# Attention then graph attention on one core: products with reciprocals last in a beat of the first element, finishes from the fourth-last chunk, two places for the rows of bv

## The chip, the cores and the metric

The kernel runs on one core of a Trainium2 chip. The metric is the device time of one execution in microseconds (us), the median of the runs; lower is better. The core has five engines that run side by side and wait for each other by semaphores: TensorE (PE, matmuls), VectorE (DVE), ScalarE (ACT), GpSimd (POOL) and SyncE (SP), which here issues every DMA. Each engine works through its instructions in the order in which the program wrote them.

## The reference

Two layers over x of shape 8 x 2048 x 256 with one 2048 x 2048 adjacency matrix. The first is attention with 4 heads of 64, in which the softmax runs within each chunk of 256 keys and the 8 chunks are added; the second is graph attention; each ends in a residual and a layer norm.

```python
# layer 0
scores = einsum('bhnd,bhjcd->bhnjc', q, kc) / sqrt(Dh)
scores = clip(scores, -10, 10)
scores = where(mask == 0, -10, scores)
attn = softmax(scores, axis=-1)              # within a chunk of 256 keys
ctx = einsum('bhnjc,bhjcd->bhnd', attn, vc)  # summed over the 8 chunks
out = layernorm(ctx @ Wo.T + bo + x) * gamma + beta
x = layernorm(x + out)
# layer 1
e = leaky_relu(s_i[:, :, None] + s_j[:, None, :], 0.2)
attention = softmax(where(mask, e, -inf), axis=-1)
x = layernorm(x + elu(attention @ Wh))
```

## The kernel before

Everything is written in float32, with the order of the instructions set by hand: an engine executes what the Python code emits, in that order.

**Tiling.** An element of the batch has 4 blocks of 512 queries, a block has 8 chunks of 256 keys, a chunk two halves of 128 keys. The main loop (L900) runs over the 256 chunks J; each half of a chunk is a *beat*, so there are 512 beats and some more for the end. An element is 64 beats.

**One beat.** `begin_beat` emits the steps of the second layer that are under way; then come the scores of the beat (L882, PE, into PSUM), the clip with the mask (L893, DVE, in place in PSUM), the exponential (L897, ACT). The scores of the next beat's first pair of heads are already emitted in this beat when there is room. Then follow the matmuls with the values for the chunk *before* (L948): in the chunk's first half the sums of the exponentials (part 2, `ds`) and the first half of the values, in its second half the rest. ACT copies them out of PSUM (L956 to `un`, L962 to `ds`). Last comes `end_beat`.

**The reciprocals' way.** `ds` goes by DMA to a narrow tile `dc` (L964), DVE takes the reciprocal (`inverse`, L970), it goes to DRAM (`rd`, L972) and back over all partitions (`spread`, `r`, L976). Then `scaled` multiplies: for chunk 0 DVE writes ctxT (L981), for the others DVE multiplies `un` in place (L983) and POOL adds it to ctxT (L984). These three are put into `agenda` for the beats in which they fall due: in the first element `inverse` and `spread` one beat after the matmuls and `scaled` four beats after them, later at once and two beats after. `un` has two places, and every third chunk of the first element uses the tile `hr` in addition.

**end_beat (L842).** Before the change, in the first element (beat < 64) and after beat 512, it first calls what is due in `agenda`, in the order in which it was put there; then it emits the products of the second layer and advances each generator in `ahead` and `fins` by one step; then it calls what is left in `agenda`. In between, so in elements 1 to 7, all that is due comes behind the generators.

**The generators.** In the first element `fins` holds the projections of keys and values, `weights_made` (L234), `masks_made` (L163), which turns the adjacency into int8 masks on DVE (L154, L157, diagonal blocks L161) and ACT (L155), and `far_made` (L193; L201, L204), which makes a bfloat16 table for the second layer. `fin` (L342) finishes a block: it loads x (L346) and in its next beat lets POOL add the biases (L349 y, L350 x); when the block's eight chunks are in ctxT (`ctx_done`), in a later beat, come the projection by Wo (L357, L364), statistics (L316 to L322), `normalize` (L329), gamma and beta (L370, L371, on DVE for the very last block), a second norm, a store and a transposition (L383). `fin` is put into `fins` by `scaled` of the chunk NCH - 3, the third-last. The prelude of the second layer for an element (L475) takes maxima over the far table (L438, DVE), with loads of 256 KB (L430). Steps of the second layer use L714 and L727 (ACT), L718 and L723 (DVE, L723 with the int8 mask), L736 (POOL) and L746 (PE). Queries for the next block are loaded (`xT_q`, L120) at the end of the second beat of chunk 6 of a block.

**bv.** In `weights_made`, bv is multiplied through Wo by two matmuls (L247) whose stationary operand is a tile `bvr` filled from bv (L246); both use the tag `hr`, which has one place.

Of the kernel before, what the change touches and what calls it, by code (L numbers as in the profile page):

```python
# [9 lines left out]
F32 = mybir.dt.float32  # L10
# [9 lines left out]
P = 128  # L20
# [8 lines left out]
def tile_adj_attention__then__gat(  # L29
# [42 lines left out]
    NIB = N // IB  # L72
    TPB = IB // P
    NPAIR = H // 2
    NCH = N // CHUNK
# [11 lines left out]
    one = ctx.enter_context(tc.tile_pool(name="one", bufs=1))  # L87
# [146 lines left out]
    def weights_made():  # L234

        for n in range(2):
            for k in range(KC):
                wa = one.tile([P, F], F32, tag="hr", name=f"wa{n}_{k}")
                nc.vector.tensor_mul(wa, W_aug[:, k, 0:F], a_bc[n])
                nc.vector.reduce_sum(W_aug[:, k, F + n : F + n + 1], wa, axis=AX.X)  # L240
            yield

        pb = ps_m.tile([P, F], F32, tag="m", name="pb")
        for k in range(KC):
            rep = one.tile([P, P], F32, tag="hr", name=f"bvr{k}")
            nc.vector.tensor_scalar(rep, ones, bv_c[:, k : k + 1], None, ALU.mult)  # L246
            nc.tensor.matmul(pb, rep, WT["o"][:, k, :], start=(k == 0), stop=(k == KC - 1))  # L247
        nc.vector.scalar_tensor_tensor(bo_bc, pb, float(NCH), bo_bc, ALU.mult, ALU.add)
# [439 lines left out]
    total = B * NIB * NCH  # L688
# [116 lines left out]
    agenda = {}  # L805
    beat = 0
# [6 lines left out]
    def at(when, fn):  # L813
        agenda.setdefault(when, []).append(fn)
# [27 lines left out]
    def end_beat():  # L842

        nonlocal weighted
        if beat < 2 * NIB * NCH or beat >= 2 * total:
            for fn in agenda.pop(beat, []):
                fn()
        for s in weighted:
            s.product()
        weighted = []  # L850
        for gens in (ahead, fins) if beat < 2 * total else (fins, ahead):
            for g in list(gens):
                if next(g, g) is g:
                    gens.remove(g)
        for fn in agenda.pop(beat, []):
            fn()
# [8 lines left out]
    qT = make_qT(0, 0, xT_kv[0, 0])  # L865
    fins.append(projections())
    fins.append(weights_made())
    fins.append(masks_made())
    fins.append(far_made())
# [30 lines left out]
    for J in range(total + 1):  # L900
        b, ib, j = J // (NIB * NCH), J // NCH % NIB, J % NCH
# [4 lines left out]
        for half in range(2):  # L906
# [30 lines left out]
            if prev is not None:  # L937
                if half == 0:

                    pool, tag = (one, "hr") if early and J % 3 == 2 else (two, "un")  # L940
                    prev["un"] = pool.tile([P, 2, IB], F32, tag=tag, name=f"un{prev['name']}")
                for part in ((2, 0), (1,))[half]:
                    m = ps_m.tile([P, IB], F32, tag="m", name=f"u{prev['name']}_{part}")
                    for i in range(2):
                        pc = 2 * prev["j"] + i
                        for h in range(H):
                            f0 = h * D + part * DH
                            nc.tensor.matmul(  # L948
                                m[h * DH : (h + 1) * DH, :],
                                prev["v"][pc // TPB][:, pc % TPB, f0 : f0 + DH] if part < 2 else ones[:, 0:DH],  # L950
                                prev["es"][2 * i + h // 2][:, h % 2, :],
                                start=(i == 0),
                                stop=(i == 1),
                            )
                    if part < 2:
                        nc.scalar.copy(prev["un"][:, part, :], m)  # L956
                    else:

                        ds = two.tile([P, IB], F32, tag="ds", name=f"ds{prev['name']}")
                        nc.scalar.copy(ds, m)  # L962
                        dc = two.tile([P, IB // DH], F32, tag="dc", name=f"dc{prev['name']}")
                        nc.sync.dma_start(  # L964
                            out=dc, in_=ds.rearrange("(h m) (n w) -> h m n w", m=DH, n=DH)[:, 0, :, :]
                        )
                        prev["dc"] = dc

                        def inverse(p=prev):
                            nc.vector.reciprocal(p["dc"], p["dc"])  # L970
                            p["rd"] = dram3.tile([H, IB], F32, tag="rd", name=f"rd{p['name']}")
                            nc.sync.dma_start(out=p["rd"].rearrange("h (m w) -> (h m) w", m=DH), in_=p["dc"])  # L972

                        def spread(p=prev):
                            p["r"] = two.tile([P, IB], F32, tag="r", name=f"r{p['name']}")
                            nc.sync.dma_start(out=p["r"], in_=p["rd"].unsqueeze(1).to_broadcast([H, DH, IB]))  # L976

                        def scaled(p=prev):
                            r2 = p["r"].unsqueeze(1).to_broadcast([P, 2, IB])
                            if p["j"] == 0:  # L980
                                nc.vector.tensor_mul(p["ctxT"], p["un"], r2)  # L981
                            else:
                                nc.vector.tensor_mul(p["un"], p["un"], r2)  # L983
                                nc.gpsimd.tensor_add(p["ctxT"], p["ctxT"], p["un"])  # L984
                            if p["j"] == NCH - 1:
                                ctx_done[p["b"], p["ib"]] = beat
                            if p["j"] == NCH - 3:
                                fins.append(fin(p["b"], p["ib"], p["ctxT"]))

                        lag = 1 if early else 0  # L990
                        at(beat + lag, inverse)
                        at(beat + lag, spread)
                        at(beat + 2 + 2 * lag, scaled)

            end_beat()
            if half == 1:

# [8 lines left out]
    while agenda or fins or ahead or l1_live or l1_open():  # L1006
        begin_beat(1.0)
        middle_of_beat()
        end_beat()
        beat += 1  # L1010
# [44 lines left out]
```

## Time and profile before

| what | value |
|---|---|
| median of 3 runs | 4391.52 us (4390.94 to 4396.86) |
| the profiled execution, whole | 4386.54 us |
| its span, first to last instruction | 4384.7 us |
| mean granted TensorE clock | 0.979 |
| L983, product, 224 times | 277.2 us busy, mean 1238 ns |
| L984, POOL's addition, 224 times | 567.9 us busy, mean 2535 ns |

By stage, from the table of busy times by window:

| us of the span | PE busy | DVE busy | POOL busy | granted clock |
|---|---|---|---|---|
| 0 to 480 (480) | 430.85 | 335.53 | 115.75 | 0.96 |
| 480 to 1000 (520) | 495.21 | 409.99 | 228.15 | 0.99 |
| 1000 to 1527 (527) | 501.88 | 417.81 | 233.78 | 0.99 |
| 2585 to 3114 (529) | 501.80 | 418.39 | 233.59 | 0.99 |
| 4120 to 4385 (265) | 182.43 | 214.56 | 54.18 | 0.85 |

How to read the lines that follow. In a timeline a row gives the start and the length in us, the engine, the source line, the operation, the tile written and those read, how often, and in brackets the engine's idle time before it with what ended it. In a table of groups the columns are busy us, mean ns of one, and idle us before with the releasers. The chain of waits is followed back from the last instruction to what released each step. A tile's buffer number is left out. PE's records are modelled to overlap, so a busy PE isn't PE at its peak. PEld is the weight load on PE. Line numbers are those of the kernel before.

### The profile page before, as it was taken

How to read it: one execution, taken by the hardware profiler on the slowest of the kernel's cores; microseconds unless marked ns; L12 is line 12 of the kernel's file. 1: busy time of each engine (PE TensorE's matmuls, PEld its weight loads, DVE VectorE, ACT ScalarE, POOL GpSimd, SP SyncE). 2: the span in 40 equal slices, each digit the busy share in tenths (PEclk: the TensorE clock that was granted, in tenths of full speed). 3: DMA queues.
4: the chain of work that ended last, by engine and by line, in shares of the span. 5: the costliest groups of instructions: out<-in, count | busy, mean ns of one | idle time of the engine just before them, and what ended most of it. 6: DMA issues, size and time to landing. Idle time of an engine off the chain costs nothing.

```text
span 4384.7 us, 61166 instructions
## 1 busy us (share of the span) xinstructions
PE 4055.8 (92%) x23053; PEld 1913.0 (44%) x23053; DVE 3417.1 (78%) x4530; ACT 2555.5 (58%) x3842; POOL 1759.3 (40%) x901
## 2 busy tenths in 40 slices
PE   8889989999899999999899998999989999899767
PEld 3223334454345534454344543445434454344456
DVE  5876589965898668976699766996579965888777
ACT  5655556665566556666566665566556665555546
POOL 0222235543455434444245442554325542354420
PEclk9999999999999999999999999999999999999889
DMA  5554232223332133321333223222232222322321
GB/s 163 172 174 149 73 114 86 84 72 95 93 97 82 56 108 102 100 75 47 108 103 98 74 74 105 83 95 80 72 105 84 89 78 65 117 83 81 123 73 58
DMA packets 257642, 415.63 MB, mean 95 GB/s; under 512 B 85441, under 2 KB 120513, under 8 KB 256449
## 3 DMA queue, kind: packets, MB, share of 16 engines
q1 hardware_dynamic: 257344, 411.71, 30.7%
q8 instruction: 181, 2.97, 0.3%
q14 instruction: 117, 0.95, 0.1%
HBM read 340.66 MB, written 68.88 MB: 93 GB/s over the span
## 4 chain that ended last, share of the span: by engine, by line
PE 57%; DVE 23%; ACT 7%; DMA 7%; issue 5%; POOL 1%; SPq 0%; DVEq 0%; ACTq 0%; POOLq 0%
PE u L948 17%; PE sc L882 14%; PE us L746 12%; DVE sc L893 6%; DVE fb L438 3%; DVE w L718 3%; PE pv L275 3%; PE pk L256 3%; ACT e L897 3%; DMA dc<-ds 2%; PE pq L256 2%; DVE w L723 2%; PE po L357 2%; PE pw L398 2%; PE us L761 1%
## 5 line engine op out<-in xcount | busy, mean ns | idle before, releaser
L893 DVE SCALAR_TENSOR_TENSOR sc<-sc,mk 128x1024 f32<-128x1024 f32 x1024 | 1205.8, 1222 | 523.1 <-PE sc L882 375.0
L897 ACT ACTIVATE e<-sc 128x1024 f32<-128x1024 f32 x1024 | 1032.7, 1021 | 951.8 <-DVE sc L893 926.5
L882 PE MATMUL sc<-qT,kT 64*128 64x512 f32 x4096 | 1038.7, 622 | 71.8 <-ACT e L897 68.6
L984 POOL TENSOR_TENSOR ctxT<-ctxT,un 128x1024 f32<-128x1024 f32 x224 | 567.9, 2535 | 1135.6 <-DVE un L983 1099.8
L948 PE MATMUL u<-e,v 128*32 128x512 f32 x8192 | 982.8, 597 | 0.0
L746 PE MATMUL us<-wh,w 128*128 128x256 f32 x3584 | 883.0, 396 | 89.5 <-ACT w L727 68.2
L746 PEld LDWEIGHTS us<-wh,w 128*128 128x128 f32 x3584 | 669.8, 194 | 432.5 <-ACT w L727 119.7
L736 POOL TENSOR_TENSOR acc<-acc,w 128x512 f32<-128x512 f32 x392 | 600.0, 1531 | 548.1 <-ACT w L727 537.6
L882 PEld LDWEIGHTS sc<-qT,kT 64*128 64x128 f32 x4096 | 344.3, 186 | 581.3 <-issue 313.7
L718 DVE SCALAR_TENSOR_TENSOR w<-ab,sj,w 128x512 f32<-128x512 f32 x512 | 576.5, 1147 | 6.1 <-ACT w L714 6.1
L948 PEld LDWEIGHTS u<-e,v 128*32 128x32 f32 x8192 | 240.6, 110 | 659.8 <-issue 500.9
L948 PE MATMUL u<-e,ones 128*32 128x512 f32 x4096 | 498.4, 605 | 0.0
L723 DVE TENSOR_TENSOR w<-w,mk 128x512 f32<-128x512 f32 x512 | 458.5, 916 | 45.6 <-DMA mk<-mask 43.1
L438 DVE CUSTOM_DVE_ANT_0 fb<-sj_row,fb 128x1024 bf16<-128x1024 f32 x240 | 383.7, 1609 | 4.5 <-DMA fb<-far 4.5
L956 ACT COPY un<-u 128x512 f32<-128x512 f32 x512 | 300.7, 587 | 108.8 <-PE u L948 100.1
L714 ACT ACTIVATE w<-ab,sj 128x512 f32<-128x512 f32 x512 | 352.3, 715 | 9.9 <-POOL acc L734 5.2
L727 ACT ACTIVATE w<-w 128x512 f32<-128x512 f32 x512 | 308.8, 629 | 83.6 <-DVE w L723 83.2
L983 DVE TENSOR_TENSOR un<-un,r 128x1024 f32<-128x1024 f32 x224 | 277.2, 1238 | 43.6 <-DMA r<-rd 23.1
L948 PEld LDWEIGHTS u<-e,ones 128*32 128x32 f32 x4096 | 107.5, 110 | 352.7 <-issue 286.5
L970 DVE RECIPROCAL dc<-dc 128x16 f32<-128x16 f32 x256 | 63.5, 248 | 149.3 <-DMA dc<-ds 137.3
L962 ACT COPY ds<-u 128x512 f32<-128x512 f32 x256 | 148.6, 580 | 18.5 <-PE u L948 15.5
L357 PE MATMUL po<-WT_o,ctxT 128*128 128x256 f32 x512 | 127.4, 405 | 33.3 <-POOL ctxT L984 29.2
(112 smaller groups left out, 3078.7 us busy)
## 6 DMA issues: line engine op xcount, KB each, us to landing
r<-rd SPq DMA_DIRECT2D x256, 256.0 KB
mk<-mask SPq DMA_DIRECT2D x120, 512.0 KB
fb<-far SPq DMA_DIRECT2D x240, 256.0 KB
xT_k<-in_xT_dram SPq DMA_DIRECT2D x32, 512.0 KB
raw<-in_adjT_dram SPq DMA_DIRECT2D x32, 512.0 KB
rawf<-in_adj_dram SPq DMA_DIRECT2D x32, 512.0 KB
x<-in_x_dram SPq DMA_DIRECT2D x32, 512.0 KB
h_d<-y SPq DMA_DIRECT2D x32, 512.0 KB
```

What stands on the lines that cost most here:

```text
L438: nc.vector.tensor_tensor_reduce(out=fb, in0=row, in1=fb, scale=1.0, scalar=2 * FAR * 0.999, op0=ALU.add, op1=ALU.max, accum_out=dst,)
L714: nc.scalar.activation(self.w, k["ab"][:, 1, :], AF.Identity, bias=k["sj"][:, 1, c : c + 1])
L718: nc.vector.scalar_tensor_tensor(self.w, k["ab"][:, 0, :], k["sj"][:, 0, c : c + 1], self.w, ALU.add, ALU.max)
L723: nc.vector.tensor_tensor(self.w, self.w, self.k["mks"][self.c // HT][:, self.c % HT, :], ALU.min)
L727: nc.scalar.activation(self.w, self.w, AF.Exp)
L736: nc.gpsimd.tensor_add(k["acc"], k["acc"], self.w)
L746: nc.tensor.matmul(k["us"][:, t, :], self.w[:, ts(t, P)], k["wh"][c // TPB][:, c % TPB, 0:F], start=(first and t % 2 == 0), stop=last, ski ...
L882: nc.tensor.matmul(sc[:, h, :], kTs[b][n // TPB][h * D : (h + 1) * D, hp, ts(n % TPB, P)], qT[h * D : (h + 1) * D, hp, :], start=True, sto ...
L893: nc.vector.scalar_tensor_tensor(sc, sc, -CLIP, cap, ALU.max, ALU.min)
L897: nc.scalar.activation(e, sc, AF.Exp)
L948: nc.tensor.matmul(m[h * DH : (h + 1) * DH, :], prev["v"][pc // TPB][:, pc % TPB, f0 : f0 + DH] if part < 2 else ones[:, 0:DH], prev["es"] ...
L984: nc.gpsimd.tensor_add(p["ctxT"], p["ctxT"], p["un"])
```

## The change

Three edits.

1. `end_beat`: in the first element what is due is split. All but `scaled` is called first, as before; the `scaled` that are due go back into `agenda` and are called by the last loop of `end_beat`, behind the generators. After beat 512 nothing changes.
2. `scaled` puts `fin` into `fins` at chunk NCH - 4 (the fourth-last). In elements 1 to 7, and for the last block of the first element, x is loaded and its biases are added two beats sooner; for the other blocks of the first element one beat sooner, since there `scaled` now runs behind the generators. The projection by Wo still waits for `ctx_done`.
3. The second `bvr` tile takes the place `ex` instead of `hr`.

```diff
@@ weights_made
-            rep = one.tile([P, P], F32, tag="hr", name=f"bvr{k}")
+            rep = one.tile([P, P], F32, tag=("hr", "ex")[k], name=f"bvr{k}")
@@ end_beat
-        if beat < 2 * NIB * NCH or beat >= 2 * total:
+        if beat < 2 * NIB * NCH:
+            now = agenda.pop(beat, [])
+            agenda[beat] = [fn for fn in now if fn.__name__ == "scaled"]
+            for fn in now:
+                if fn.__name__ != "scaled":
+                    fn()
+        elif beat >= 2 * total:
             for fn in agenda.pop(beat, []):
                 fn()
@@ scaled
-                            if p["j"] == NCH - 3:
+                            if p["j"] == NCH - 4:
                                 fins.append(fin(p["b"], p["ib"], p["ctxT"]))
```

## The prediction

> **What bounds the kernel now.** I read the page first: its totals and its chain.
>
> ```profile
> PE 4055.8 (92%) x23053; PEld 1913.0 (44%) x23053; DVE 3417.1 (78%) x4530; ACT 2555.5 (58%) x3842; POOL 1759.3 (40%) x901
> ...
> PE 57%; DVE 23%; ACT 7%; DMA 7%; issue 5%; POOL 1%; SPq 0%; DVEq 0%; ACTq 0%; POOLq 0%
> ```
>
> TensorE (PE) carries most of the chain, so a gain has to come out of its idle time or out of the stretches where VectorE (DVE) takes its place. The table of stages says where idle time is: in the first 480 us PE is busy for 430.85 us (49 us idle), in the later elements for about 500 of 527, in the last 265 us for 182. The change touches the first, little of the middle, and the entry to the last.
>
> Second, the groups of the first 520 us, shapes kept apart:
>
> ```profile
> L893 DVE SCALAR_TENSOR_TENSOR sc<-sc,mk 128x1024 f32<-128x1024 f32 x153 | 180.3, 1224 | 95.7 <-PE sc L882 95.1
> ...
> L984 POOL TENSOR_TENSOR ctxT<-ctxT,un 128x1024 f32<-128x1024 f32 x31 | 79.8, 2576 | 296.2 <-DVE un L983 285.5 <-ACT ds L962 10.6
> ...
> L157 DVE TENSOR_SCALAR mb<-raw 128x1024 int8<-128x1024 int32 x32 | 49.9, 1559 | 0.0
> ```
>
> L157 has a median of 0.68 us (its line by itself) and a mean of 1.56, so 49.9 - 32 x 0.68 = 28 us are stretch. The clip L893 never exceeds 1.233 us in 1024 runs. The timeline shows what stretches L157:
>
> ```profile
> 192.40 1.22 DVE L983 TENSOR_TENSOR un<-un,r 128x1024 f32<-128x1024 f32 x1
> ...
> 193.53 0.69 DVE L154 TENSOR_SCALAR mk<-raw 128x1024 int8<-128x1024 int32 x1
> 193.69 2.74 POOL L984 TENSOR_TENSOR ctxT<-ctxT,un 128x1024 f32<-128x1024 f32 x1 [4.67 <-DVE un L983]
> ...
> 194.14 2.85 DVE L157 TENSOR_SCALAR mb<-raw 128x1024 int8<-128x1024 int32 x1
> ...
> 199.04 2.37 DVE L893 SCALAR_TENSOR_TENSOR sc<-sc,mk 128x1024 f32<-128x1024 f32 x2
> ...
> 200.31 1.02 ACT L897 ACTIVATE e<-sc 128x1024 f32<-128x1024 f32 x1 [3.99 <-DVE sc L893]
> ...
> 201.38 2.08 PE L882 MATMUL sc<-qT,kT 64*128 64x512 f32 x4 [3.89 <-ACT e L897]
> ```
>
> The product L983 releases GpSimd's (POOL's) addition L984; the mask instruction behind it ends only when that addition does, 2.17 us late; the next clip is late, its exponential, and PE waits 3.89 us.
>
> **Part 1: products last in a beat, first element.** The instruction lists of the two kernels, built from the code, are the same on PE and ScalarE (ACT). On DVE some 25 products move behind the masks, far rows and statistics of their beat, so the next DVE instructions are the two clips (2.35 us), in whose shadow L984 (2.35 to 2.7 us) fits. What PE idle time goes, by the groups of its gaps that follow a stretched instruction:
>
> - Gaps ending at 196.37 and 201.38 (0.91 + 3.89), one L157 stretched: 2.2. Gaps at 297.53 and 302.30 (0.79 + 3.64), one L157: 2.2.
> - Gaps at 247.81 and 253.85 (0.31 + 4.91): here L154 (2.84), L157 (2.86) and L161 (2.51) are stretched by L349, L350 and L984, 6.4 us in all. Gaps at 350.5 and 354.0 (2.41 + 2.33): L983 (3.30), L154 (2.85), L157 (2.83), again 6.4. The finish now begins one beat sooner there, so L349 and L350 run in a beat that has no mask work; a product or a mask instruction can still meet them. Between 2.2 and the whole gaps (5.2 and 4.7): 3.3 each.
> - Block 0's finish, gaps of 0.76, 1.41 and 0.87 near 139.8 to 156.3: between 0 and 3.0, I take 2.0.
> - The finish of the element's last block moves two beats: PE idles 2.08 us before L357 at 471.17, while POOL goes from L350 (ends 464.3) through two additions. That goes: 2.1.
>
> Sum 2.2 + 2.2 + 3.3 + 3.3 + 2.0 + 2.1 = 15.1.
>
> Behind a gap PE also runs slower:
>
> ```profile
> 245.57 1.92 PE L948 MATMUL u<-e,v 128*32 128x512 f32 x16
> ...
> 253.85 2.08 PE L882 MATMUL sc<-qT,kT 64*128 64x512 f32 x4 [4.91 <-ACT e L897]
> 255.86 3.64 PE L948 MATMUL u<-e,ones 128*32 128x512 f32 x16
> ```
>
> Sixteen matmuls take 3.64 us instead of 1.92; the granted clock is 0.66 in 250 to 260, and 0.57, 0.57, 0.62 behind the other three pairs of gaps. That is about 1.7 us each, 6.9 for four, if all four gaps fall under what triggers it, 0 if none: I take 3.0. The Trainium skill, "TensorE: Matmul & The Clock Gate", Part 1, puts the half rate behind an idle window of about 3.4 us; by that the shortened gaps would cost nothing, the term would be 6.9 and the whole sum 29. The trace disagrees: a gap of 2.08 us is followed by 0.72 over 470 to 476.
>
> Against it: the last product of block 0 now stands behind L154 and L157 (0.63 + 0.67), and PE already waits there for L984 (1.04 us before 161.5): +1.3. The later L984 also frees its `un` place later by up to 4 us; that place is needed a beat and more later (three in turn in this element), so 0; without that cover ACT's copy L956 and PE's `u` would stand still for the same 4 us. The reciprocals L970 keep their place, and so their waits for dc (18.0 us, 7 times).
>
> Another page speaks against the part: "GPSIMD Engine Reference", section 1 (Specifications), says that GpSimd shares its SBUF interfaces with VectorE and collides with two-input instructions, so the moved product itself stays exposed. The trace has it, but seldom (L983 at most 3.37 us, median 1.215); by the rule three such hits would take 3 x 2.1 = 6.3 off, and the sum would be 19.
>
> **Part 2: bv rows.** DVE waits 4.44 us at 35.65 for the first matmul L247. Now its second row is made at once. PE waited 0.38 for it, so 0.4 is gained, and no more, since the DVE sum L248 behind needs both matmuls.
>
> **Part 3: finishes two beats sooner, elements 1 to 7.** Nothing is added; on SP the load of x (512 KB) passes the load of xT_q, and on POOL L349 and L350 pass one L984 and two or three L736. L349 waits for x on POOL (86.3 us, 9 times, after the first element); behind it now stands an L984 whose `un` place ACT writes again 11 us or more after the addition in the trace, so the 5.6 us of L349 and L350 fit, and an L736, which frees one of five `w`.
>
> Block 0 of an element is where PE idles before L357:
>
> ```profile
> 1616.29 3.25 POOL L350 TENSOR_TENSOR x<-x,beta_bc 128x1024 f32<-128x1024 f32 x1
> ...
> 1617.24 3.38 DVE L438 CUSTOM_DVE_ANT_0 fb<-sj_row,fb 128x1024 bf16<-128x1024 f32 x1
> ...
> 1624.07 1.23 DVE L438 CUSTOM_DVE_ANT_0 fb<-sj_row,fb 128x1024 bf16<-128x1024 f32 x1 [1.17 <-DMA fb<-far]
> ...
> 1630.13 6.19 PE L357 MATMUL po<-WT_o,ctxT 128*128 128x256 f32 x15 [4.26 <-POOL ctxT L984]
> ```
>
> Two beats sooner DVE has only clips and small copies, so the stretch of 2.16 us goes. But DVE then waits for the far block instead (its wait of 1.17 grows), so I don't count that. What counts is the x load that now no longer stands in front of dc: DVE waits 1.9, 1.5, 4.1, 1.9, 4.2 us there in the five blocks where the profile names dc, against 1.5 without such a load (546.06): 0.4 + 0 + 2.6 + 0.4 + 2.7 = 6.1, of which I take 4.0. Bounds: 0, and 7 x 2.16 = 15 if the far block isn't the limit.
>
> Blocks 1 to 3: L349 and L350 stretch two L723 (1.4 + 2.2 us) per block, before and after alike, 2 beats apart. PE is busy 129 of 136, 138 of 142, 129 of 133 us there, and covers it: 0. Uncovered, six blocks in the stretch where DVE is busy 15.00 of 15 us would cost 6 x 3.6 = 22; a gain of up to 8 is open too (1.31 us of PE before L357 in six third blocks). Two loads in front of dc: it is issued 5.7 us behind xT_q, x alone lands in 4.1; 0, bound +8.
>
> The last block counts in full, because from 4118 on DVE is the chain:
>
> ```profile
> 4123.48 3.33 POOL L349 TENSOR_TENSOR y<-x,bo_bc 128x1024 f32<-128x1024 f32 x1
> ...
> 4124.54 2.82 DVE L718 SCALAR_TENSOR_TENSOR w<-ab,sj,w 128x512 f32<-128x512 f32 x1
> ...
> 4126.89 2.67 POOL L350 TENSOR_TENSOR x<-x,beta_bc 128x1024 f32<-128x1024 f32 x1
> ...
> 4127.39 2.71 DVE L723 TENSOR_TENSOR w<-w,mk 128x512 f32<-128x512 f32 x1
> ```
>
> Against medians of 0.74 and 0.68 that is 2.1 + 2.0 = 4.1. Two beats sooner DVE sits idle for 6.60 us (before L408 at 4108.88) and PE is the chain, which covers both. I take 4.0; bounds 0, and 5 with the 1.3 us by which x delays dc there (3.06 us in the chain against some 1.8).
>
> **Sum.** -15.1 - 3.0 + 1.3 - 0.4 - 4.0 - 4.0 = -25.2 us. The profiled execution took 4386.5 (span 4384.7), which gives 4361.3. The median of the runs is 4391.5, 5.0 above it, so the forecast for the runs is 4366.
>
> **Rivals.** No change that can be told (within 8.8 us, 0.2%): the gaps refill. For it: PE also waits for xT_q (3.9 + 2.9 + 1.8) and DVE for dc in the first element, and neither moves; two 2.2 us terms, bv and half the tail remain, less 1.3: about -6, 4386. Against it: at 199 to 201 no other releaser is close behind the clip. Larger gain: every group of gaps with its slow clock (5.2 + 4.7 + 4.8 + 4.4 + 3.0 + 2.1 + 6.9 = 31), 15 in the first blocks, 5 at the end: -50, 4341. Slower: L349 and L350 of the second blocks land in the full DVE stretch of the third (22 us), while the first element gives only 4: +18, 4409; it decides from the point where clips, not PE, end last there. For it: DVE 15.00 of 15 in three slices; against: PE is 15.00 in the same ones. That products don't move is excluded by the lists.
>
> **Chances.** Forecast (a gain of 9 to 38 us) 0.58, larger 0.13, no change 0.16, slower 0.13: faster 0.71, same 0.16, slower 0.13. The forecast's own range is 4354 to 4382; to leave out no more than 2 in 10 I take 4338 to 4397.
>
> **What would show it.** L157's mean in the first 520 us near 0.7 with L984 under L893; PE's waits for ACT e in the first 480 us down from 24.1 to about 10; the clock there above 0.96; L718 and L723 unstretched near 4120; the wait before L357 in first blocks hardly smaller. It is wrong if L983 is stretched instead, or if PE's idle time in the third blocks grows.

## The result, and the profile after

The changed kernel is slower, by little: 4398.82 us (4392.37 to 4406.95, 22 runs) against 4393.18 us (4382.87 to 4397.04, 22 runs) of the kernel before on the same chip, a ratio of 1.0015 (95% interval 1.0008 to 1.0021). The forecast was 4366, faster. The profiled execution took 4397.48 us, its span is 4395.7 (before 4386.54 and 4384.7).

The page of the changed kernel, its totals and chain, shows how little the whole says:

```profile
PE 4059.2 (92%) x23053; PEld 1918.3 (44%) x23053; DVE 3376.7 (77%) x4530; ACT 2557.7 (58%) x3842; POOL 1754.2 (40%) x901
...
PE 56%; DVE 22%; ACT 8%; DMA 8%; issue 5%; POOL 1%; SPq 0%; DVEq 0%; ACTq 0%; POOLq 0%
```

DVE is busy 40 us less (3417.1 before): much of the stretch is gone, and the kernel is not faster for it. Where the time went is read by stages. Each column below is a difference between starts of clips in the timeline: up to the first clip of element 1, from there to its second block, from there to the fourth block of element 7, and from there to the end (0.3 us ahead of the span's, in every run). From `end_beat` on the changed kernel's line numbers are seven higher: L983 is now L990 (product), L984 L991, L970 L977, L956 L963, L893 L900, L897 L904.

| us | first element | first block of el. 1 | to block 4 of el. 7 | rest | end |
|---|---|---|---|---|---|
| before | 442.6 | 111.4 | 3425.0 | 405.5 | 4384.4 |
| changed | 433.3 | 116.5 | 3442.7 | 402.8 | 4395.4 |
| difference | -9.3 | +5.2 | +17.7 | -2.7 | +11.0 |

These are one execution each; the medians differ by 5.6. The first element and the last block gained, and everything between lost.

**First element.** The groups of DVE in the first 520 us of the changed kernel (busy us, mean ns | idle before):

```profile
L990 DVE TENSOR_TENSOR un<-un,r 128x1024 f32<-128x1024 f32 x31 | 41.9, 1353 | 7.0 <-DMA r<-rd 7.0
L157 DVE TENSOR_SCALAR mb<-raw 128x1024 int8<-128x1024 int32 x32 | 26.1, 816 | 0.0
```

DVE's wait for dc in the same stretch (us, times, longest), changed kernel first, then the kernel before:

```profile
DVE dc L977 <- DMA dc<-ds: 36.8, 17, 5.0
```

```profile
DVE dc L970 <- DMA dc<-ds: 21.5, 9, 3.4
```

L157 fell from 1559 to 816 ns, and the product is hardly stretched in its stead (in the first 480 us its mean was 1319 ns and is 1367). But DVE now waits 15.3 us longer for dc. Why that costs is seen at the place which the prediction priced with 0.79 + 3.64 us, in the timeline of the changed kernel:

```profile
297.03 0.25 DVE L977 RECIPROCAL dc<-dc 128x16 f32<-128x16 f32 x1 [2.49 <-DMA dc<-ds]
297.20 0.63 DVE L154 TENSOR_SCALAR mk<-raw 128x1024 int8<-128x1024 int32 x1
...
297.75 0.68 DVE L157 TENSOR_SCALAR mb<-raw 128x1024 int8<-128x1024 int32 x1
...
299.28 2.35 DVE L900 SCALAR_TENSOR_TENSOR sc<-sc,mk 128x1024 f32<-128x1024 f32 x2
...
303.96 1.94 PE L383 MATMUL pt<-ident,y 128*128 128x128 f32 x8 [4.68 <-ACT ds L969]
```

No mask instruction is stretched, but the reciprocal in front of them waits 2.49 us for its DMA, the clip comes at 299.28, and PE waits 4.68 us, a step later than before and for ACT's copy L969. So one wait takes the place of another: in the first 450 us PE's waits for ACT's `e` fell from 24.1 to 9.2 us, while those of L383 for ACT's copy `ds` rose from nothing to 6.9 and those of L357 for POOL from 1.0 to 3.9.

**Start of element 1.** Timeline of the changed kernel:

```profile
439.08 2.34 POOL L349 TENSOR_TENSOR y<-x,bo_bc 128x1024 f32<-128x1024 f32 x1 [11.15 <-DMA x<-in_x_dram]
441.50 2.34 POOL L350 TENSOR_TENSOR x<-x,beta_bc 128x1024 f32<-128x1024 f32 x1
443.80 2.34 POOL L991 TENSOR_TENSOR ctxT<-ctxT,un 128x1024 f32<-128x1024 f32 x1
446.17 0.58 ACT L963 COPY un<-u 128x512 f32<-128x512 f32 x1 [8.68 <-POOL ctxT L991]
446.81 3.78 PE L256 MATMUL pk<-xT_k,WT_k 128*128 128x512 f32 x4 [6.38 <-ACT un L963]
```

POOL waits 11.15 us for x, which was issued at 431.54 and landed 7.5 us later. The addition L991 stands behind; ACT's copy waits 8.68 us for its `un` place, PE 6.38 for ACT. Before, L349 came behind that addition (459.46), and ACT waited 3.01. By beat 2 of element 1, 8.15 of the 9.3 us are lost.

**Elements 1 to 7.** In beat 15 of blocks 1 and 2 (counted from 0) of most elements 1 to 4 us are lost. One of them:

```profile
2773.56 2.35 POOL L349 TENSOR_TENSOR y<-x,bo_bc 128x1024 f32<-128x1024 f32 x1 [1.85 <-PE u L955]
2774.45 4.80 DVE L723 TENSOR_TENSOR w<-w,mk 128x512 f32<-128x512 f32 x2
...
2775.99 2.71 POOL L350 TENSOR_TENSOR x<-x,beta_bc 128x1024 f32<-128x1024 f32 x1
...
2782.20 2.35 DVE L900 SCALAR_TENSOR_TENSOR sc<-sc,mk 128x1024 f32<-128x1024 f32 x2
...
2785.50 0.58 ACT L963 COPY un<-u 128x512 f32<-128x512 f32 x1
...
2786.13 3.29 PE L256 MATMUL pq<-xT_q,WT_q 128*128 128x512 f32 x4 [2.14 <-ACT un L963]
```

Two L723 take 4.80 us next to the two additions (1.28 at 2767.20 in the kernel before). DVE has no pause from there to the clip at 2782.20, so the clip, the exponentials and ACT's copy behind them are late, and PE waits in front of the next queries; the four matmuls behind the wait take 3.29 us instead of 1.98. Over the run the matmuls of L256 waited 36.0 us for ACT's copy `un` (27 times), in the kernel before 12.4 (19); 6.4 of it is the wait at the start of element 1.

**Last block.** L349 and L350 left the two instructions that the prediction named, but met another L723, and the next addition met an L718:

```profile
4114.97 3.46 DVE L723 TENSOR_TENSOR w<-w,mk 128x512 f32<-128x512 f32 x2
4115.50 2.37 POOL L349 TENSOR_TENSOR y<-x,bo_bc 128x1024 f32<-128x1024 f32 x1 [2.67 <-DMA x<-in_x_dram]
...
4135.18 3.38 POOL L991 TENSOR_TENSOR ctxT<-ctxT,un 128x1024 f32<-128x1024 f32 x1 [2.08 <-DVE un L990]
4136.26 2.85 DVE L718 SCALAR_TENSOR_TENSOR w<-ab,sj,w 128x512 f32<-128x512 f32 x1
```

### The profile page after: what moved, and what is told of

Same layout as the page of the kernel before. It is cut to its first block, busy times and chain, and to the rows that moved or that the text cites. A ratio compares the mean times of both kernels' runs of the same rounds, so it can differ in the third digit from the quotient of the medians.

```text
span 4395.7 us, 61109 instructions
## 1 busy us (share of the span) xinstructions
PE 4059.2 (92%) x23053; PEld 1918.3 (44%) x23053; DVE 3376.7 (77%) x4530; ACT 2557.7 (58%) x3842; POOL 1754.2 (40%) x901
## 4 chain that ended last, share of the span: by engine, by line
PE 56%; DVE 22%; ACT 8%; DMA 8%; issue 5%; POOL 1%; SPq 0%; DVEq 0%; ACTq 0%; POOLq 0%
PE u L955 17%; PE sc L889 14%; PE us L746 12%; DVE sc L900 6%; DVE w L718 3%; DMA dc<-ds 3%; DVE fb L438 3%; PE pk L256 3%; DVE w L723 3%; ACT e L904 3%; PE pv L275 2%; PE po L357 2%; PE pq L256 2%; PE pw L398 2%; DMA mk<-mask 2%
## 5 line engine op out<-in xcount | busy, mean ns | idle before, releaser
L900 DVE SCALAR_TENSOR_TENSOR sc<-sc,mk 128x1024 f32<-128x1024 f32 x1024 | 1206.2, 1222 | 513.4 <-PE sc L889 367.4
L904 ACT ACTIVATE e<-sc 128x1024 f32<-128x1024 f32 x1024 | 1032.1, 1020 | 931.6 <-DVE sc L900 906.4
L991 POOL TENSOR_TENSOR ctxT<-ctxT,un 128x1024 f32<-128x1024 f32 x224 | 557.8, 2490 | 1110.5 <-DVE un L990 1092.3
L736 POOL TENSOR_TENSOR acc<-acc,w 128x512 f32<-128x512 f32 x392 | 598.7, 1527 | 546.8 <-ACT w L727 536.8
L718 DVE SCALAR_TENSOR_TENSOR w<-ab,sj,w 128x512 f32<-128x512 f32 x512 | 572.9, 1140 | 6.2 <-ACT w L714 6.1
L723 DVE TENSOR_TENSOR w<-w,mk 128x512 f32<-128x512 f32 x512 | 452.9, 906 | 42.8 <-DMA mk<-mask 40.2
L438 DVE CUSTOM_DVE_ANT_0 fb<-sj_row,fb 128x1024 bf16<-128x1024 f32 x240 | 368.5, 1545 | 25.0 <-DMA fb<-far 25.0
L963 ACT COPY un<-u 128x512 f32<-128x512 f32 x512 | 300.6, 587 | 119.9 <-PE u L955 104.2
L714 ACT ACTIVATE w<-ab,sj 128x512 f32<-128x512 f32 x512 | 351.9, 713 | 11.4 <-POOL acc L734 5.5
L990 DVE TENSOR_TENSOR un<-un,r 128x1024 f32<-128x1024 f32 x224 | 278.7, 1244 | 43.7 <-DMA r<-rd 26.3
L977 DVE RECIPROCAL dc<-dc 128x16 f32<-128x16 f32 x256 | 63.6, 248 | 162.5 <-DMA dc<-ds 159.0
L357 PE MATMUL po<-WT_o,ctxT 128*128 128x256 f32 x512 | 133.1, 419 | 43.1 <-POOL ctxT L991 43.1
L256 PE MATMUL pq<-xT_q,WT_q 128*128 128x512 f32 x248 | 126.3, 646 | 38.3 <-ACT un L963 28.4
```

Source lines behind the costliest of these rows:

```text
L256: nc.tensor.matmul(pm, WT[name][:, k, ts(o, P)], xt[:, k, :], start=(k == 0), stop=(k == KC - 1))
L438: nc.vector.tensor_tensor_reduce(out=fb, in0=row, in1=fb, scale=1.0, scalar=2 * FAR * 0.999, op0=ALU.add, op1=ALU.max, accum_out=dst,)
L714: nc.scalar.activation(self.w, k["ab"][:, 1, :], AF.Identity, bias=k["sj"][:, 1, c : c + 1])
L718: nc.vector.scalar_tensor_tensor(self.w, k["ab"][:, 0, :], k["sj"][:, 0, c : c + 1], self.w, ALU.add, ALU.max)
L723: nc.vector.tensor_tensor(self.w, self.w, self.k["mks"][self.c // HT][:, self.c % HT, :], ALU.min)
L736: nc.gpsimd.tensor_add(k["acc"], k["acc"], self.w)
```

## The experiments

All compute the whole reference. T is the beat in which a finish (of blocks 0 to 2 of the first element) loads x in the kernel before; the changed kernel does so at T-1.

| kernel | first element: due last, finish | el. 1 to 7 | first element | first block | middle | rest | ratio to before (95%) |
|---|---|---|---|---|---|---|---|
| before | nothing, T | before | 442.6 | 111.4 | 3425.0 | 405.5 | 1 |
| changed | products, T-1 | early | 433.3 | 116.5 | 3442.7 | 402.8 | 1.0015 (1.0008 to 1.0021) |
| e1_last | products, T+1 | before | 453.2 | 109.2 | 3421.1 | 405.9 | 1.0020 (1.0011 to 1.0029) |
| e2_fin4 | nothing, T-2 | early | 431.2 | 109.0 | 3441.2 | 402.7 | 1.0005 (0.9996 to 1.0014) |
| e4_el0 | products, T-1 | before | 433.0 | 110.8 | 3419.8 | 405.0 | 0.9971 (0.9960 to 0.9983) |
| e5_hold | products, T-1 | x early | 434.1 | 108.4 | 3415.1 | 404.3 | 0.9961 (0.9948 to 0.9973) |
| e8_lastT | products, T | before | 439.1 | 110.9 | 3426.7 | 404.6 | 0.9984 (0.9975 to 0.9993) |
| e9_oldT1 | nothing, T-1 | before | 434.0 | 109.0 | 3428.4 | 405.0 | 0.9984 (0.9975 to 0.9993) |
| e6_un | products, T-1 | early | 432.4 | 107.8 | 3437.9 | 403.1 | 0.9999 (0.9988 to 1.0010) |
| e10_both | nothing, T-2 | x early | 437.3 | 108.8 | 3416.2 | 404.9 | 0.9964 (0.9951 to 0.9978) |
| e11_alllast | all, T-1 | x early | 419.1 | 108.5 | 3416.7 | 406.5 | 0.9915 (0.9902 to 0.9929) |
| e12_tail | products, T-1 | x early, last block early | 434.6 | 108.4 | 3416.6 | 405.2 | 0.9945 (0.9931 to 0.9959) |
| e13_mid | products, T-1 | held in blocks 1, 2 only | 437.5 | 108.4 | 3421.1 | 402.7 | 0.9953 (0.9940 to 0.9965) |
| e14_sooner | all, T-2 | x early, last block early | 421.5 | 108.4 | 3414.3 | 405.1 | 0.9915 (0.9902 to 0.9929) |

"Early" is x and additions two beats sooner, "x early" x alone. The middle column groups cleanly: five executions with the finish of before, 3419.8 to 3428.4 (mean 3424.2); three with the early one, 3437.9 to 3442.7 (3440.6); five with x early and additions held, 3414.3 to 3416.7 (3415.8). The first column scatters more: the six kernels with products last at T-1 lie between 432.4 and 437.5.

**e1_last: edit 1 alone.** The kernel before with the changed `end_beat`.

> The kernel before with edit 1 alone (products last in a beat in the first element; finishes still begin at the third-last chunk, so in the first element one beat later than before; both bvr tiles in hr). Theory: the loss of the changed kernel comes from edit 2, edit 1 gains. Start of element 1 some 8 to 10 us sooner than in the kernel before, no loss in beats 0 to 2 of element 1 (GpSimd finds no 11 us wait for x there), no step at beat 15 of blocks 1 and 2 later; total 7 to 11 us below the kernel before, ratio 0.9975 to 0.9985. Rival: the moved products are paid back within the first element and edit 2 is neutral; then the ratio is 1.000 or above, and the start of element 1 is no more than 3 us sooner.

A miss of the theory: edit 1 alone loses 10.6 us in the first element. Since the finish is put into `fins` by `scaled`, which now runs behind the generators, L349 and L350 come a beat later, and into the mask work; timeline of this kernel:

```profile
256.43 2.36 POOL L349 TENSOR_TENSOR y<-x,bo_bc 128x1024 f32<-128x1024 f32 x1 [14.68 <-issue]
256.68 2.65 DVE L154 TENSOR_SCALAR mk<-raw 128x1024 int8<-128x1024 int32 x1
258.87 2.67 POOL L350 TENSOR_TENSOR x<-x,beta_bc 128x1024 f32<-128x1024 f32 x1
259.26 2.83 DVE L157 TENSOR_SCALAR mb<-raw 128x1024 int8<-128x1024 int32 x1
```

Both mask instructions are stretched again, now by the finish. The beat of the finish had to be separated from the order of the products.

**e2_fin4: edit 2 alone.** The kernel before with NCH - 4.

> The kernel before with edit 2 alone (finishes of all blocks begin at the fourth-last chunk, products of the first element in their old place). Theory: all of the loss is here. The first beats of element 1 lose 6 to 9 us behind GpSimd's wait for x, beat 15 of blocks 1 and 2 of elements 1 to 7 loses 1 to 4 us each, part of it given back in the next block, some 12 us in all, the tail gives back 3 to 4: 12 to 18 us above the kernel before, ratio 1.003 to 1.004. Rival (edit 1 is what loses): ratio within 0.9995 to 1.001.

Half right: the loss in elements 1 to 7 is edit 2's (3441.2). The ratio, 1.0005, lies in the range of the rival, though, because the first element gains 11.4 us, with products in their old place, and the start of element 1 loses next to nothing (0.6): there x is loaded one beat sooner than in the changed kernel. The loss at that start needs both edits together.

**e4_el0: early finish in the first element only.**

```diff
-                            if p["j"] == NCH - 4:
+                            if p["j"] == (NCH - 4 if p["b"] == 0 and p["ib"] < NIB - 1 else NCH - 3):
```

> The changed kernel with finishes at the fourth-last chunk only in blocks 0 to 2 of the first element, at the third-last everywhere else. Theory: the start of element 1 is about 9 us sooner than in the kernel before and the distance stays so to the end, since from there both issue the same order: ratio 0.9975 to 0.9985. Rival: the drift in elements 1 to 7 is not of edit 2's making (it follows from how the first element ends, or is scatter of the executions): the distance shrinks by 10 us or more on the way to element 7.

As the theory said (the ratio, 0.9971, is a little better than its range), and the middle is that of the kernel before: the drift is edit 2's making in elements 1 to 7.

**e5_hold: x early, additions held.**

```diff
         yield
+        if b > 0 or ib == NIB - 1:
+            yield
+            yield
         y = one.tile([P, TPB, F], F32, tag="y", name=f"y{b}_{ib}")
```

> The changed kernel, x loaded two beats sooner as in it, but GpSimd's two additions L349 and L350 held back by two beats, so that they stand where the kernel before has them (from the last block of the first element on). Theory: what costs is where the two additions run, at the start of element 1 as an in-order wait in front of an addition into ctxT, later as stretched L723 in a beat in which VectorE is full. Both go: no wait of more than 2 us for x on GpSimd in front of an addition, PE's idle time before pq in beat 15 of blocks 1 and 2 back to about 4 us in sum (22 in the changed kernel), ratio 0.997 to 0.999. Rival: what costs is the x load two beats sooner (on SP ahead of xT_q and dc); then beat 15 loses as in the changed kernel, and the ratio is 1.000 to 1.002.

The theory held, and more than that: the middle falls to 3415.1, below the kernel before. There, x comes so late in the first blocks that L349 runs into L438. First the kernel before, then e5_hold (whose L352 is L349), the same block of element 5:

```profile
2673.99 2.36 POOL L349 TENSOR_TENSOR y<-x,bo_bc 128x1024 f32<-128x1024 f32 x1 [14.91 <-DMA x<-in_x_dram]
2674.93 2.50 DVE L438 CUSTOM_DVE_ANT_0 fb<-sj_row,fb 128x1024 bf16<-128x1024 f32 x1
2676.43 3.24 POOL L350 TENSOR_TENSOR x<-x,beta_bc 128x1024 f32<-128x1024 f32 x1
...
2677.36 3.38 DVE L438 CUSTOM_DVE_ANT_0 fb<-sj_row,fb 128x1024 bf16<-128x1024 f32 x1
```

```profile
2646.89 2.35 POOL L352 TENSOR_TENSOR y<-x,bo_bc 128x1024 f32<-128x1024 f32 x1
2649.33 2.35 POOL L353 TENSOR_TENSOR x<-x,beta_bc 128x1024 f32<-128x1024 f32 x1
```

With x there in time the additions wait for nothing and are over before L438 begins. So loading x early is worth some 8 us in elements 1 to 7 (3424.2 to 3415.8), of which places like this one have the smaller part (see the next section), and the additions in beat 14 cost some 25 (3415.8 to 3440.6).

**e8_lastT and e9_oldT1: order and beat apart.** Both from e4_el0: e8 with one `yield` ahead of the load in blocks 0 to 2 of the first element (T), e9 with the same `yield` and the old `end_beat` (T-1).

> Products last in the first element, but finishes of its blocks 0 to 2 begin in the same beat as in the kernel before (T); elsewhere the third-last chunk as before. With the kernel before (old order, T), the next run (old order, T-1) and e4_el0 (products last, T-1) this is a table of two by two. Measured so far, at the start of element 1 against the kernel before: old order at T-2 -11.4, last at T-1 -9.3 to -9.7, last at T+1 +10.6. Theory now: the beat in which L349 and L350 run decides, and the order of the products is worth next to nothing: -3 to +3 here. Rival, the prediction's term: the order alone brings most of it: -7 to -12.

> Old order of the products, finishes of blocks 0 to 2 of the first element one beat sooner than before (T-1), elsewhere as before. Theory: -7 to -12 at the start of element 1, like e4_el0 which differs only in the order. Rival, the prediction's term: the one beat brings little, -3 to +1. If both e8_lastT and e9_oldT1 gain half, the two add up.

The beat alone brings -8.6, the order alone -3.5 (just past the bound that was set), and both together -5.1 to -10.3 in the six kernels, -8.5 on average: by these single executions, no more than the beat. The medians don't say so: e8 and e9 have a ratio of 0.9984 each, and e4, with both, has 0.9971 (0.9960 to 0.9983), which fits a plain sum. Part of the scatter is TensorE's clock. At the end of block 1 PE waits for the next queries `xT_q`, and the matmuls behind that wait run fast or slow; the kernel before, then the changed one:

```profile
224.45 3.67 PE L256 MATMUL pq<-xT_q,WT_q 128*128 128x512 f32 x8 [2.90 <-DMA xT_q<-in_xT_dram]
```

```profile
224.25 6.57 PE L256 MATMUL pq<-xT_q,WT_q 128*128 128x512 f32 x8 [3.91 <-DMA xT_q<-in_xT_dram]
```

The granted clock from 215 to 235 us is 1.00 in the first and 0.83 in the second. The same eight matmuls take 5.37 us in e9 and 6.04 in e8, where those one block later take 5.37 as well (3.67 before); so e8 lost some 4 us in this way and e9 1.7. Whether the order adds some us to the beat stays open.

Split between beats of the first element (change against before, us; 1.3 is beat 3 of block 1), the four show what adds and what is given back:

| from, to | e9: T-1 | e8: order | changed: both | e11: all last, T-1 |
|---|---|---|---|---|
| start to 1.0 | -3.0 | -1.6 | -1.7 | -6.4 |
| 1.0 to 1.3 | +2.0 | -0.7 | +2.1 | -0.7 |
| 1.3 to 1.6 | -0.1 | -2.7 | -2.6 | -6.3 |
| 1.6 to 1.11 | 0.0 | +1.5 | +1.5 | -1.0 |
| 1.11 to 2.0 | +2.0 | +3.2 | +3.4 | +3.2 |
| 2.3 to 2.6 | -3.4 | -2.8 | -6.3 | -8.3 |
| 2.6 to 3.0 | -1.0 | +1.3 | -0.4 | +3.5 |
| 3.3 to 3.6 | -5.2 | -1.5 | -5.1 | -7.4 |

(2.0 to 2.3, 3.0 to 3.3 and 3.6 to the end change by 0.1 at most.) Of the two gaps with L349 and L350 in them, the one at 2.3 closes in part under either edit and further under both, and the one at 3.3 under the beat alone as far as under both. What the order gives from 1.3 to 1.6 is returned from 1.6 to 2.0. Of the 3.4 us that the changed kernel loses from 1.11 to 2.0, 2.9 are the slower matmuls shown above; e11, which waits less for dc, loses 3.2 there, too.

**e6_un: one more `un` place.**

```diff
-                    pool, tag = (one, "hr") if early and J % 3 == 2 else (two, "un")
+                    pool, tag = (one, "hr") if (early or J == NIB * NCH) and J % 3 == 2 else (two, "un")
```

> The changed kernel with one more un tile in hr (the one of the last chunk of the first element). Theory: the 8 us lost in beats 0 to 2 of element 1 are ACT's copy waiting for the un place behind GpSimd's wait for x, so they go: the start of beat 2 stays 8 to 10 us sooner than in the kernel before instead of 1, GpSimd's wait for x stays near 11 us, and the ratio falls by 0.002 to 0.9995. Rival: PE or ACT waits for something else that is late there (kT, the product into ctxT), and 5 us or more of the loss stay.

The loss at the start of element 1 is gone whole (first block 107.8), with POOL's wait for x still there:

```profile
437.45 2.35 POOL L349 TENSOR_TENSOR y<-x,bo_bc 128x1024 f32<-128x1024 f32 x1 [10.49 <-DMA x<-in_x_dram]
437.46 3.70 PE L256 MATMUL pk<-xT_k,WT_k 128*128 128x512 f32 x8
437.65 0.59 ACT L963 COPY un<-u 128x512 f32<-128x512 f32 x1 [1.14 <-PE u L955]
```

ACT no longer waits for POOL, and the matmuls `pk` run through. It was the `un` place.

**e10_both: old order, x early everywhere.** e5_hold's hold for elements 1 to 7, the old `end_beat`, NCH - 4 everywhere.

> Finishes at the fourth-last chunk everywhere, products in their old order, both bvr tiles apart, and L349 and L350 held back by two beats in elements 1 to 7. Theory: -11 us at the start of element 1 as in e2_fin4, no loss at beat 15 later, and the x load two beats sooner brings what it brought in e5_hold (-10 more): 18 to 24 us below the kernel before, ratio 0.9945 to 0.996. Rival: e5_hold's further gain in elements 1 to 7 is scatter of one execution; then 11 to 15 us, 0.9965 to 0.9975.

Middle 3416.2 as in e5_hold, so that gain isn't scatter. The first element missed the theory, -5.3 instead of -11, and the ratio, 0.9964, lies between the two ranges. It took 437.3 where e2_fin4, of the same order there but for the bvr place, took 431.2: 6 us lie within the scatter of one execution, 5.5 of it just ahead of blocks 2 and 3, where PE waits 1.3 and 1.0 us longer for `xT_q` and the eight matmuls behind that wait take 5.37 us in e10 and 3.67 in e2, both times.

**e11_alllast: reciprocals last, too.**

```diff
         if beat < 2 * NIB * NCH:
-            now = agenda.pop(beat, [])
-            agenda[beat] = [fn for fn in now if fn.__name__ == "scaled"]
-            for fn in now:
-                if fn.__name__ != "scaled":
-                    fn()
+            pass
```

(on e5_hold; within a beat, the first element then has the order of the later ones.)

> As e5_hold (x loaded early, additions held back), but in the first element everything due, so the reciprocals and their DMAs too, comes last in the beat. Theory: the gap that the products left is refilled by VectorE's wait for dc in front of the mask work (2.49 us at 297.03 in the changed kernel, dc waits of the first 520 us up from 21.5 to 36.8 us). With the reciprocals behind the mask work that wait shrinks to 15 us or less, and the start of element 1 is 3 to 7 us sooner than in e5_hold (434.1). Rival: the loop from the sums to r is what is late; put later still, r misses its product, VectorE waits for r instead, and the start of element 1 is the same or up to 8 us later.

The theory was right in sign and too small: the first element takes 15.0 us less than in e5_hold. DVE's waits in the first 520 us, e5_hold, then e11_alllast:

```profile
DVE dc L980 <- DMA dc<-ds: 38.4, 19, 4.8
```

```profile
DVE dc L976 <- DMA dc<-ds: 23.4, 13, 4.8
```

The wait falls by the same 15.0 us, not to the 15 us expected. The place shown for the changed kernel at 297 us, in e11_alllast:

```profile
282.24 0.68 DVE L157 TENSOR_SCALAR mb<-raw 128x1024 int8<-128x1024 int32 x1
...
282.84 0.68 DVE L201 TENSOR_SCALAR mf<-rawf 128x1024 bf16<-128x1024 int32 x1
...
283.78 0.24 DVE L976 RECIPROCAL dc<-dc 128x16 f32<-128x16 f32 x1
283.94 2.33 DVE L899 SCALAR_TENSOR_TENSOR sc<-sc,mk 128x1024 f32<-128x1024 f32 x2
```

The mask work now runs while dc is on its way, and the reciprocal waits for nothing.

**e12_tail, e13_mid, e14_sooner.** e12 holds the additions back except in the last block; e13 only in blocks 1 and 2 (and in the last of the first element); e14 is e11_alllast with NCH - 5 and a `yield` in the first element (T-2), last block not held.

> As e5_hold, but the last block's additions are not held back. This measures the prediction's term for the last block by itself. The stretch from the fourth block of element 7 to the end took 405.2 us on average with the finish of before, 402.9 with the early one, 404.3 and 404.9 with early load and late additions. Theory: 402.5 to 403.2 here, so 2 us and not 4, and the ratio 0.9955 to 0.9965. Rival: the tail is scatter, 404 to 405.

> As e5_hold, but additions are held back only in blocks 1 and 2 of elements 1 to 7 and in the last block of the first. Theory: only there do L349 and L350 fall into beat 14 with VectorE full of L723 and the next queries behind it; in blocks 0 and 3 beat 14 has room. The stretch from the second block of element 1 to the fourth of element 7 takes 3412 to 3420 us (3425.0 before, 3442.7 in the changed kernel, 3415.1 and 3416.2 with all held back), the tail 402.5 to 403.2, the ratio 0.9955 to 0.9965. Rival: the four blocks share the loss; then the stretch is 3425 or more.

> As e11_alllast, with finishes of blocks 0 to 2 of the first element one beat sooner still (T-2), and the last block's additions not held back. Two places, read apart in the trace. Theory: with everything due last, PE's gaps in the first element that L349 and L350 had a part in are gone already (e11_alllast has none left at beats 3 to 5), so the start of element 1 stays within 3 us of 419.1; the last block's part from its eighth beat to the end falls from 338.0 to 333.5 to 335.5. Ratio 0.9905 to 0.992. Rival: the beat of L349 and L350 still counts as it did with old order (-8.6 at T-1, -5.3 to -11.4 at T-2): start of element 1 at 413 to 416, ratio below 0.990.

e12's rest is 405.2, a miss by the numbers set. Its beat 7 came 1.7 us late; from the eighth beat to the end the early last block took 334.0 and 333.6 (changed, e2), 334.3, 334.3, 335.1 (e6, e13, e12) and 336.6 (e14, outside what was expected), on average 334.7; the eight others took 335.9 to 338.0, on average 336.8. So the early last block is worth about 2 us, within a scatter of 1 to 3. e13's middle is 3421.1, below the rival's 3425 and just above the range set: blocks 1 and 2 carry most of the loss, whether all of it stays open. e14's first element is 2.4 us longer than e11's, as the theory allowed: once all is due last, an earlier finish brings nothing more.

e11_alllast and e14_sooner beat both kernels: 4356.14 us (4 runs) against 4393.28, and 4353.57 (5 runs) against 4390.48, both 0.9915 (0.9902 to 0.9929), some 37 us below the kernel before.

## Why the prediction was wrong, point by point

By stages, forecast and measured: the first element -17.2 and -9.3 us, elements 1 to 7 with their start -4.0 and +22.9, the last stretch -4.0 and -2.7.

**"Sum 2.2 + 2.2 + 3.3 + 3.3 + 2.0 + 2.1 = 15.1", with 3.0 for the clock.** L157 lost most of its stretch as forecast, and over the stretches of the table above the changed kernel gains 16.3 us in all. What failed was to count next to nothing (1.3) behind the gaps: in three of the stretches it gives 7.0 back, so 9.3 are left. The step that failed is the sentence "The reciprocals L970 keep their place, and so their waits for dc (18.0 us, 7 times)". They keep their place, but not their waits: the product used to stand in front of them and the beat was longer, so dc had more time; now, in the first 520 us, they wait 36.8 us in 17 waits (21.5 in 9 before), in front of the mask work. e11_alllast against e5_hold shows what that costs, and the traces of all 14 kernels agree: in the first 450 us DVE waits for dc 18 to 23 us in the four with the old order, 31 to 35 in the eight with the products alone last, and 16 to 17 in the two with all that is due last.

A second wait refills as well: when PE is sooner at the end of block 1, it waits longer for `xT_q` (2.90 to 3.91 us), and the slower clock behind that costs 2.9 us. The clock of the first 480 us went from 0.96 to 0.97 only, so the 3.0 for the clock is not seen. The rival "no change" named both waits, and the forecast gave neither a price.

**Which edit brings it.** The prediction put the two groups with L349 and L350 at 3.3 each, though the finish's new beat was stated. Those stretches gained 6.3 and 5.1, and e9 (beat alone) has 3.4 and 5.2 there: undersized, and for the larger part the finish's doing, not the products'. Over the whole first element, what edit 1's order brings once the finish is earlier, with the reciprocals left in front, doesn't show against the scatter of single executions; by the medians some us are possible.

**Block 0's last product, +1.3.** There is a loss there (2.1 from 1.0 to 1.3), but e9 with the old order has it (2.0), and e8 with the new one hasn't: it comes with the finish at T-1.

**`un` place in the first element, "so 0"; POOL in elements 1 to 7, "the 5.6 us of L349 and L350 fit".** Wrong at the seam of the two, where the third place is no longer used and x is not there yet. The sum took the additions' own 5.6 us and left out the wait for x in front of them (11.15 us): 8.15 us lost. e6_un removed it by a place alone.

**bv, -0.4.** Right: between two clips around it the changed kernel takes 10.35 us, the one before 11.00, so -0.65.

**First blocks of elements 1 to 7, -4.0.** The sign was right and the reason wrong. DVE's wait for dc hardly moved (105.6 us from 550 to 3980 before, 113.2 in the changed kernel, 107.4 in e5_hold). What the early x removes is POOL's wait for it (86.3 us in 9 waits, none in e5_hold), and with it the stretched L438. That "I don't count that" held for the most part: of 11.9 us of PE's idle time in beats 2 and 3 of the blocks that follow, 8.1 came back before `po` in beat 4. By the starts of clips (means of the five kernels with the finish of before and of the five with x early and the additions held) these beats 1 and 2 gain 25.8 us over the elements and beats 3 and 4 return 23.0, so 2.8 of the 8.4 us of the middle column lie here. Of the rest, 1.9 lie in beat 12 of the first blocks and 2.8 where the third blocks pass into the fourth (8.6 lost in beats 14 and 15, 11.4 gained in the beat behind them); what frees PE there was not tested and stays open.

**Blocks 1 to 3, "PE ... covers it: 0".** This is the largest error: the early additions cost some 25 us in the middle against x early alone, 16 against the kernel before. The rows quoted (PE busy 129 of 136 us and the like) span many beats; the one beat that the additions go to, beat 14 with DVE full and the next queries behind it, wasn't read by itself. The rival "slower" had the mechanism, though in the beats of the next block, and priced it at 22; it got 0.13 because PE was full in the same slices. That was no reason against it: a PE that is full on average still waits where a single clip comes late.

**Last block, -4.0.** Right in sign, half the size, about -2: L718 is met by the next addition instead.

The parts of the profiled executions close: -9.3 + 5.2 + 17.7 - 2.7 = +10.9, against 11.0 between the spans.

## What to carry to other kernels

When one instruction is moved behind others, look at what becomes first in its place: an in-order engine that waited behind a stretched instruction may wait for a DMA instead, so move the whole group that hangs on the DMA, not one member. Price a moved step with the rows of the beat it goes to, not of the beat it leaves, and count its own wait (here for x) as time that everything behind it in the queue will wait. A load and the work that needs it can be moved apart: loading early paid, adding early cost three times as much.

## What the runs showed of the hardware

- Tiny DVE instructions are stretched next to POOL as well: in the changed kernel L453 on 128 x 4 elements takes 148 ns at the least and 1224 in the median (1240 at most), beside an L736 of POOL in the case seen:

```profile
2784.44 3.18 POOL L736 TENSOR_TENSOR acc<-acc,w 128x512 f32<-128x512 f32 x2
...
2785.06 1.23 DVE L453 TENSOR_TENSOR mx<-m 128x4 f32<-128x4 f32 x1
```

  The Trainium skill, "GPSIMD Engine Reference", section 1 (Specifications), names such contention for DVE instructions with two SBUF inputs; this row agrees for an instruction of hardly any work, while the clip, which reads PSUM and a mask, again averages 1222 ns over 1024 runs.
- A load of 512 KB (x), issued 1.1 us behind a load of r and 0.5 us behind a write to far of 256 KB each, let POOL start 7.5 us later (431.54 to 439.08).
- In the first element eight matmuls `pq` behind a wait for `xT_q` took 3.67 us in 12 of the 14 cases with a wait below 3 us, and 5.08 to 6.68 us in 27 of the 28 with a longer one (14 traces); the shortest wait with slow matmuls behind it is 2.10 us, the longest with fast ones 3.57.
- Executions of one order differ by 5 to 6 us at the end of the first element (432.4 to 437.5 with products last at T-1, 431.2 and 437.3 in e2 and e10), by 8.6 in the middle stretch with the finish of before (3419.8 to 3428.4), and by 2.4 there with x early and the additions held (3414.3 to 3416.7).
